# A four-layer graph network on one core: layer 3 in one-pass matmuls behind a run-time check of the adjacency

## The chip, the cores and the metric

The kernel runs on one core of one Trainium2 chip. The metric is device microseconds for one execution. The profile is one further execution, recorded by the hardware profiler; its span is the time between its first and last instruction. Engines are named as in the profile: PE (matrix multiply), PEld (its weight loads), DVE (vector), ACT (scalar, with function tables), POOL (GpSimd) and SP (a queue that issues transfers).

## The reference

A feature matrix x (2708 nodes, 128 features) goes through four graph layers, each on the layer-normed, clipped features and added back to x. The adjacency `adj` is 2708 by 2708 in fp32; it is drawn at random and holds only 0 and 1. Layer 0 is a masked attention, layer 1 a normalised sum over neighbours, layer 2 a mean over neighbours with a batch norm. Layer 3 is the one that the change is about:

```
XW = h @ W ;  s_col = XW @ a[:f] ;  s_row = XW @ a[f:]
den = exp(leaky_relu(s_row[:, None] + s_col[None, :], 0.01))
num = A @ den
att = where(num != 0, den / num, 0)
out = x + A @ (att @ XW)
```

So layer 3 has a product of the adjacency with a 2708 by 2708 matrix, a logarithm and an exponential over all of it, a product with XW, and a last product with the adjacency. The kernel is handed the adjacency as it is (`adj`) and transposed (`adj_t`).

## The kernel before

**Tiles.** Nodes lie in T = 22 tiles of 128 (the last has 20). A row tile of the adjacency is 128 x 2708 fp32, 1354 KB. Columns are worked on in six blocks `E0`: five of 512 and one of 148, each in its own PSUM bank. `product` (layers 1, 2 and the end of 3) walks over the 22 row tiles: for each one, `aggregate` (L209) multiplies the tile by a 128 x 128 stationary matrix into the six banks. The last four tiles (`NLAST`) are walked block by block, so that the `finish` function of a block can begin while the next block is multiplied. Row tiles are fetched by SP into a ring of buffers, so SP waits only for a free buffer.

**Layer 3, tables (L445 to L941).** The kernel does not form the product A @ den row by row. It sorts the nodes by s_row into chunks and the columns by s_col, because inside a chunk the leaky ReLU has one slope. From comparisons, ranks and one-hot matrices (DVE, some PE) it makes index tables: `row_i` (which rows of `adj_t` a step needs), `pre_i` (which pre-summed rows), `xw_i` (which rows of XW). `sums` (L640) streams all 22 tiles of `adj_t` and forms running sums of whole chunks, which are written to DRAM as `pre_d`. `densities` (L910 to L925) fills `dmat`, which holds 44 matrices of 128 x 128.

**Layer 3, the loop (L943 to L990).** It has NE = 22 steps. A step s has two halves. For each half, `fetch` lets POOL gather 126 rows of `adj_t` into partitions 0 to 125 (L457, index `row_i`) and 2 rows of `pre_d` into partitions 126 and 127. The buffers `rows` come from the pool `steps`, which has four. For each of the six blocks, PE multiplies `dmat` of both halves by the two row buffers into a bank (L980), and there are two such banks in turn. ACT takes Ln of the bank (L984), DVE subtracts that from `e` in three pieces (L986), and ACT then takes Exp of all of `e` (L988). `e` itself was begun by DVE at L975, in a buffer that is free once `spread_values` of two steps earlier has read it. `spread_values(s - 1)` (L962) multiplies the `e` of the step before by its gathered XW rows into six accumulators. The order on PE is held by hand: L980 of step s, then L962 of step s - 1.

**Layer 3, the end (L993 to L1030).** The accumulators are turned by PE and scaled into `hn` (L1002); then `product` runs once more over the 22 tiles of `adj_t` with `hn` as the stationary side, and `finish3` adds to x and stores the result.

All matmuls on fp32 data are plain fp32 ones. Each appears in the profile as two records.

Of the kernel before, what the change touches and what calls it, by code (L numbers as in the profile page):

```python
# [10 lines left out]
I32 = mybir.dt.int32  # L11
AF = mybir.ActivationFunctionType
# [5 lines left out]
def kernel(  # L18
# [187 lines left out]
    def aggregate(stationary, moving, accs, start, stop, blocks=range(NB)):  # L206
        for b in blocks:
            lo, hi = E0[b]
            nc.tensor.matmul(accs[b][:, : hi - lo], stationary, moving[:, lo:hi], start=start, stop=stop)  # L209
# [13 lines left out]
    with ExitStack() as stack:  # L223
# [168 lines left out]

        def load_with_turn(t):
            a = kept[t] if t in kept else load_rows(adj, t)
            if t not in kept and turns:
                b = turns.pop(0)
                p = bank()
                turned(p, h2, TILES[b])
                nc.vector.tensor_copy(hT[:, spans(b)], p[:, : len(TILES[b]) * P])
            return a  # L400
# [11 lines left out]
        product(order2, lambda t: h2[:, t, :], load_with_turn, range(NB), finish2)  # L412
        nc.vector.bn_aggr(tot[:, 0:2], st2)
# [15 lines left out]
    CH = P - 2  # L429
# [6 lines left out]
    pre_d = dram.tile([2 * NC, N], F32, name="pre_d")  # L436
# [14 lines left out]
    pre_i = keepers.tile([P, NS], I32, name="pre_i")  # L451
    c_rel = keepers.tile([P, NE], F32, name="c_rel")
    c_exp = keepers.tile([P, NE], F32, name="c_exp")
    r_exp = keepers.tile([P, T], F32, name="r_exp")

    def gather(out, src, idx):
        return nc.gpsimd.indirect_dma_start(  # L457
            out=out,
            out_offset=None,
            in_=src,  # L460
            in_offset=bass.IndirectOffsetOnAxis(ap=idx, axis=0),
        )

# [3 lines left out]
    with tc.tile_pool(name="tab", bufs=1) as tab, tc.tile_pool(name="tabs", bufs=2) as tabs:  # L467
# [27 lines left out]
        nc.vector.memset(first[0:1, :], 1.0)  # L495
        slope_hi = const.tile([P, 1], F32, name="slope_hi")
        nc.vector.tensor_scalar(slope_hi, part, float(CH), -0.99, ALU.is_equal, ALU.mult)
        nc.vector.tensor_scalar_add(slope_hi, slope_hi, 1.0)
        slope_lo = const.tile([P, 1], F32, name="slope_lo")
        nc.vector.tensor_scalar(slope_lo, part, float(CH + 1), 0.99, ALU.is_equal, ALU.mult)  # L500
        nc.vector.tensor_scalar_add(slope_lo, slope_lo, 0.01)
# [371 lines left out]
        nc.vector.tensor_copy(row_i, pick("row_f", ktab[:, NC:]).rearrange("p e h -> p (e h)"))  # L873
        chunk = pick("chunk", lane[:, :NC])
# [19 lines left out]
        first_rows = (hT, row_b)  # L894
        for h in range(2):
            gather(first_rows[h][:CH, :N], adj_t[:, :], row_i[:CH, h : h + 1])

# [29 lines left out]
        for s0 in range(0, FIRST, 4):  # L927
            densities(s0)
        for t in range(NEARLY, T):
            sums(t)  # L930
        for s0 in range(FIRST, NS, 4):
            densities(s0)
        pre_sb = hn.rearrange("p t d -> p (t d)")[:, : 3 * BW].rearrange("p (b i) -> p b i", i=BW)
        with tc.high_priority():
            for b in range(3):
                w = BLK[b][1] - BLK[b][0]
                nc.scalar.copy(pre_sb[: 2 * NC, b, :w], accs[b][: 2 * NC, :w])
                nc.vector.tensor_copy(pre_sb[64 : 64 + 2 * NC, b, :w], accs[b][64 : 64 + 2 * NC, :w])
            flat = hn.rearrange("p t d -> p (t d)")
            for h, queue in enumerate((nc.sync, nc.scalar)):  # L940
                queue.dma_start(pre_d[:, h * HALF : (h + 1) * HALF], flat[64 * h : 64 * h + 2 * NC, :HALF])  # L941

    with tc.tile_pool(name="att", bufs=2) as attp:  # L943

        accs = [acc_bank(b) for b in range(NB)]
        done = {}

        def fetch(s):
            if s < 2:
                a = first_rows[s][:, :N]  # L950
            else:
                a = steps.tile([P, N], F32, tag="rows", name="rows")
                one = gather(a[:CH, :], adj_t[:, :], row_i[:CH, s : s + 1])
                if s < 6:
                    tc.keep_in_program_order(one)
            gather(a[CH:, :], pre_d[:, :], pre_i[0:2, s : s + 1])
            return a
# [7 lines left out]
        for s in range(NE):  # L965
            a2 = [fetch(2 * s + h) for h in range(2)]
            if s >= 3:
                fetch_xw(s)
            xw = xw_s[s % 4]
            m = nc.vector.tensor_scalar_mul(xw, xw, c_exp[:, s : s + 1])  # L970
            if s < 4:
                tc.keep_in_program_order(m)
            e = attp.tile([P, N], F32, tag="e", name="e")
            ln = attp.tile([P, N], F32, tag="ln", name="ln")
            nc.vector.tensor_scalar(e, row_a[:, :N], c_rel[:, s : s + 1], 0.0, ALU.add, ALU.max)  # L975
            beg = 0
            for b, (lo, hi) in enumerate(E0):
                num = bank()
                for h in range(2):
                    m = nc.tensor.matmul(  # L980
                        num[:, : hi - lo], dmat[:, 2 * s + h, :], a2[h][:, lo:hi], start=(h == 0), stop=(h == 1)
                    )
                    tc.keep_in_program_order(m)
                nc.scalar.activation(ln[:, lo:hi], num[:, : hi - lo], AF.Ln, bias=tiny)  # L984
                if b in (2, 4, 5):
                    nc.vector.tensor_sub(e[:, beg:hi], e[:, beg:hi], ln[:, beg:hi])  # L986
                    beg = hi
            nc.scalar.activation(e, e, AF.Exp)  # L988
            done[s] = (xw, e)
            if s:  # L990
                spread_values(s - 1)
        spread_values(NE - 1)


    scale = small.tile([P, T], F32, tag="scale", name="scale")
    nc.vector.scalar_tensor_tensor(scale, deg, 0.0, r_exp, ALU.not_equal, ALU.mult)
    for b in range(NB):
        evacuate(b, yT, accs[b])
        p = bank()
        turned(p, yT, TILES[b], True)  # L1000
        for q, t in enumerate(TILES[b]):
            nc.vector.tensor_scalar_mul(hn[:, t, :], p[:, cols(q)], scale[:, t : t + 1])  # L1002


    late = ctx.enter_context(tc.tile_pool(name="late", bufs=3))
    pools = [steps] * 4 + [late] * 3

    def finish3(b, acc):
        evacuate(b, yT, acc)
        p = bank()  # L1010
        turned(p, yT, TILES[b], True)
        t0 = TILES[b][0]
        f = len([t for t in TILES[b] if t < TF])
        nc.vector.tensor_add(
            xs[:, t0 : t0 + f, :].rearrange("p t d -> p (t d)"),
            xs[:, t0 : t0 + f, :].rearrange("p t d -> p (t d)"),
            p[:, : f * P],
        )
        nc.sync.dma_start(
            out[t0 * P : (t0 + f) * P, :].rearrange("(t p) d -> p t d", p=P), xs[:, t0 : t0 + f, :]  # L1020
        )
        if f < len(TILES[b]):
            nc.vector.tensor_add(xs[:TAIL, TF, :], xs[:TAIL, TF, :], p[:TAIL, cols(f)])
# [37 lines left out]
```

## Time and profile before

| | us |
|---|---|
| median of 3 runs | 1044.93 (1042.61 to 1044.98) |
| the profiled execution | 1046.11 |
| its span | 1044.3 |
| layer 3 loop, first L980 to last L962 | 613.7 to 934.2 |
| end of layer 3, after the loop | 934.2 to 1044.3 |
| mean granted PE clock | 0.972 |

The page gives the busy time of each engine, the same in 40 slices, the transfers, the chain that ended last, and the costliest groups of instructions. A group's row has the line, the engine, the operation, output and inputs by name, shapes and count; then busy microseconds in all, mean nanoseconds of one, and the idle time of that engine just before them with what ended it. A busy PE is not PE at its peak: records overlap, so a mean of one record is longer than the distance between two.

### The profile page before, as it was taken

The page shows a single profiled execution, that of the slowest core. Times are in us where ns is not written, and L with a number is a line of the kernel's source. Part 1 is how long each engine was busy: PE and PEld are TensorE (multiplying, and loading weights), DVE is VectorE, ACT ScalarE, POOL GpSimd, SP SyncE. Part 2 cuts the span into 40 slices and gives each one's busy share as a digit, 9 for nine tenths or more (in the row PEclk, how much of TensorE's full clock was granted, in tenths as well). Part 3 has the DMA queues.
Part 4 walks back from the last instruction along what each step waited for, and adds up shares of the span by engine and source line. Part 5 has one row for each costly group of instructions (what it writes and reads, how often), then busy time and mean ns, then how long its engine had stood idle before and what let it go on. Part 6 is the DMA issues. An engine that isn't in the chain of part 4 may idle for free.

```text
span 1044.3 us, 8022 instructions
## 1 busy us (share of the span) xinstructions
PE 956.5 (92%) x2850; PEld 426.0 (41%) x2850; DVE 461.3 (44%) x869; ACT 440.4 (42%) x579; POOL 165.3 (16%) x156
## 2 busy tenths in 40 slices
PE   4699999999999999966697768999999999999998
PEld 3333333344454544442232123444444444444444
DVE  5799889660004100269787242333333333340002
ACT  4579775230005000168402665665656666640000
POOL 3000001020002000020002041444334443200000
PEclk9899999999999999988899889999999999999999
DMA  8257445258865683074069744655556655569841
GB/s 300 94 213 266 175 165 192 55 225 310 309 229 205 221 302 123 0 320 162 1 257 360 198 163 177 218 192 187 183 200 218 216 181 193 198 249 369 312 170 53
DMA packets 36426, 213.06 MB, mean 204 GB/s; under 512 B 8043, under 2 KB 16923, under 8 KB 17363
## 3 DMA queue, kind: packets, MB, share of 16 engines
q1 hardware_dynamic: 21223, 146.96, 38.0%
q0 software_dynamic: 9152, 62.46, 17.0%
q10 hardware_dynamic: 6011, 3.14, 1.2%
q8 instruction: 22, 0.36, 0.1%
q14 instruction: 18, 0.14, 0.0%
HBM read 209.23 MB, written 3.32 MB: 204 GB/s over the span
## 4 chain that ended last, share of the span: by engine, by line
PE 77%; DVE 9%; ACT 7%; DMA 3%; issue 2%; POOL 1%; ACTq 0%; DVEq 0%; POOLq 0%
PE acc L209 37%; PE bank L980 16%; PE acc L962 10%; PE bank L301 7%; ACT L984 3%; DMA rows<-in_adj_t_dram 2%; PE acc L640 2%; ACT ln L984 1%; POOL rstd L160 1%; DVE bits L577 1%; PE bank L185 1%; DVE st L171 1%; ACT row_a L580 1%; PE bank L917 1%; PE acc L252 1%
## 5 line engine op out<-in xcount | busy, mean ns | idle before, releaser
L980 PE MATMUL bank<-rows,dflat 128*128 128x512 f32 x504 | 201.7, 550 | 10.6 <-ACT ln L984 10.6
L980 PEld LDWEIGHTS bank<-rows,dflat 128*128 128x128 f32 x504 | 90.6, 191 | 119.7 <-issue 91.5
L986 DVE TENSOR_TENSOR e<-e,ln 128x1536 f32<-128x1536 f32 (+2 forms) x66 | 70.5, 1097 | 145.3 <-ACT ln L984 145.3
L984 ACT ACTIVATE ln<-bank,tiny 128x512 f32<-128x512 f32 x132 | 79.4, 634 | 83.4 <-PE bank L980 83.2
L962 PE MATMUL acc<-e,xw 128*128 128x512 f32 (+1 forms) x264 | 103.4, 542 | 0.0
L209 PE MATMUL acc<-rows,hn 128*128 128x512 f32 (+1 forms) x264 | 101.7, 542 | 0.0
L209 PE MATMUL acc<-a,hn 128*128 128x512 f32 (+1 forms) x264 | 100.9, 542 | 0.0
L209 PE MATMUL acc<-a,hs 128*128 128x512 f32 (+1 forms) x228 | 88.1, 542 | 0.0
L286 ACT ACTIVATE tau<-row_a,e_neg,e_lo 128x1536 f32<-128x1536 f32 (+1 forms) x44 | 65.0, 1509 | 37.3 <-PE bank L301 27.4
L204 ACT COPY yT<-acc 128x512 f32<-128x512 f32 x9 | 5.2, 581 | 178.4 <-PE acc L209 174.9
L301 PE MATMUL bank<-tau,pick 128*6 128x512 f32 x180 | 72.6, 542 | 0.0
L962 PEld LDWEIGHTS acc<-e,xw 128*128 128x128 f32 x264 | 48.7, 190 | 52.6 <-issue 47.6
L209 PEld LDWEIGHTS acc<-a,hn 128*128 128x128 f32 x264 | 47.0, 190 | 50.2 <-issue 50.0
L209 PEld LDWEIGHTS acc<-rows,hn 128*128 128x128 f32 x264 | 46.8, 190 | 49.0 <-issue 48.8
L457 POOL DMA_INDIRECT rows<-in_adj_t_dram,row_i x42 | 41.9, 998 | 154.2 <-PE bank L980 147.8
L209 PE MATMUL acc<-yT,hs 128*128 128x512 f32 x132 | 57.6, 574 | 7.8 <-DVE yT L292 7.8
L289 DVE SCALAR_TENSOR_TENSOR tau<-tau,e_hi,a 128x1536 f32<-128x1536 f32 (+1 forms) x38 | 60.5, 1623 | 3.0 <-ACT tau L286 3.0
L975 DVE TENSOR_SCALAR e<-row_a,c_rel 128x2708 f32<-128x2708 f32 x22 | 35.8, 1630 | 57.3 <-PE acc L962 57.2
L209 PEld LDWEIGHTS acc<-a,hs 128*128 128x128 f32 x228 | 41.2, 190 | 45.4 <-issue 45.4
L640 PE MATMUL acc<-rows,wts 128*44 128x452 f32 (+1 forms) x216 | 49.3, 568 | 9.5 <-DMA rows<-in_adj_t_dram 9.4
L457 POOL DMA_INDIRECT xw<-xw_d,xw_i x22 | 41.2, 1873 | 93.7 <-DVE xw_i L841 87.3
L209 PE MATMUL acc<-row_b,hs 128*128 128x512 f32 x132 | 55.5, 553 | 0.0
(343 smaller groups left out, 1048.9 us busy)
## 6 DMA issues: line engine op xcount, KB each, us to landing
a<-in_adj_dram SPq DMA_DIRECT2D x38, 1354.0 KB, 6.5
rows<-in_adj_t_dram SPq DMA_DIRECT2D x38, 1354.0 KB, 7.2
a<-in_adj_t_dram SPq DMA_DIRECT2D x21, 1354.0 KB, 5.8
keep<-in_adj_dram SPq DMA_DIRECT2D x2, 1354.0 KB, 5.8
dflat<-in_adj_t_dram SPq DMA_DIRECT2D x2, 1354.0 KB
xw_d<-hs ACTq DMA_DIRECT2D x1, 1408.0 KB
row_a<-rdeg_d ACTq DMA_DIRECT2D x1, 1354.0 KB
yT<-in_adj_t_dram SPq DMA_DIRECT2D x1, 1354.0 KB, 5.6
```

The costliest lines, as they stand in the source:

```text
L160: nc.gpsimd.tensor_tensor(dst, s[:, :n], neg_half[:, :n], ALU.pow)
L209: nc.tensor.matmul(accs[b][:, : hi - lo], stationary, moving[:, lo:hi], start=start, stop=stop)
L286: nc.scalar.activation(tau[:, :w], row_a[:, h0:h1], AF.Relu, bias=e_neg[:, t : t + 1], scale=e_lo[:, t : t + 1])
L289: nc.vector.scalar_tensor_tensor(tau[:, :w], tau[:, :w], e_hi[:, t : t + 1], a[:, h0:h1], ALU.add, ALU.mult)
L301: nc.tensor.matmul(den[: len(E0), : hi - lo], pick[:, b, :], tau[:, lo - h0 : hi - h0], start=(ndone == 0), stop=(t == T - 1 and b == NB - 1),
L457: return nc.gpsimd.indirect_dma_start(out=out, out_offset=None, in_=src, in_offset=bass.IndirectOffsetOnAxis(ap=idx, axis=0),)
L640: nc.tensor.matmul(accs[b][64 * h : 64 * h + 2 * NC, : hi - lo], wts[:, t, :], a[:, lo:hi], start=(t == 0), stop=(t == T - 1),)
L962: m = nc.tensor.matmul(accs[b][:, : hi - lo], xw, e[:, lo:hi], start=(s == 0), stop=(s == NE - 1))
L975: nc.vector.tensor_scalar(e, row_a[:, :N], c_rel[:, s : s + 1], 0.0, ALU.add, ALU.max)
L980: m = nc.tensor.matmul(num[:, : hi - lo], dmat[:, 2 * s + h, :], a2[h][:, lo:hi], start=(h == 0), stop=(h == 1))
L984: nc.scalar.activation(ln[:, lo:hi], num[:, : hi - lo], AF.Ln, bias=tiny)
L986: nc.vector.tensor_sub(e[:, beg:hi], e[:, beg:hi], ln[:, beg:hi])
```

## The change

1. **A check.** In layer 2's product, each tile of `adj` is also put through `low_bits`: DVE masks the low 12 bits of every word, and ACT sums them into a column of `low`. `low` is reduced during layer 3's tables to `flag`, 0 if all low bits are zero.
2. **A branch.** `flag` is read into a register by every engine ahead of layer 3's loop. If it is 1, `rest(False, ...)` runs; that is the loop and the end of layer 3 in fp32. Otherwise `rest(True, ...)` runs.
3. **One-pass matmuls with halves.** In `rest(True)`, `dmat` of each half is split by DVE into `d_hi` and `d_lo`, both of type float32r (a 32-bit type that the PE multiplies with fewer mantissa bits); the rows are float32r too, and L980's product becomes two float32r matmuls per half. `hn` is split likewise into `y_hi` and `y_lo` for the last product, and each streamed tile of it is copied by DVE into a float32r buffer (`halved`). L962 stays fp32.
4. **Rows.** A half has 124 rows of `adj_t` and 4 of `pre_d` (the pre-summed rows now come in a high and a low part, `pre_hi` and `pre_lo`, made by DVE). The 124 rows are gathered as 112 and 12, with `row_j` (filled by one small transfer on ACT's queue) as the index of the 12. In `rest(True)`, POOL gathers straight into the float32r buffers; only the first four halves are gathered in fp32 into `hT`, `row_b`, `hs` and `yT` ahead of the branch, and copied by `halved`.
5. **Order in the loop.** Rows for step s + 1 are asked for in step s. After each Exp stands a one-column Ln, `again`, which nothing reads. `ln` has one buffer instead of two.

Compiled, the instructions of both sides of the branch follow each other in each engine's program, the fp32 side first.

```diff
     def aggregate(stationary, moving, accs, start, stop, blocks=range(NB)):
+        parts = stationary if isinstance(stationary, list) else [stationary]
         for b in blocks:
             lo, hi = E0[b]
...
+            for i, w in enumerate(parts):
...
+        def low_bits(t, a):
+            junk = (yT, row_b)[t % 2][:, :N]
+            bits = junk.bitcast(I32)
+            m = nc.vector.tensor_scalar(bits, a.bitcast(I32), 0xFFF, None, ALU.bitwise_and)
+            n = nc.scalar.activation(junk, bits, AF.Identity, accum_out=low[:, t : t + 1])
...
-    CH = P - 2
+    CH = P - 4
...
+    def gather_rows(a, s):
+
+        gather(a[:EVEN, :], adj_t[:, :], row_i[:EVEN, s : s + 1])
+        return gather(a[EVEN:CH, :], adj_t[:, :], row_j[: CH - EVEN, s : s + 1])
...
+                high_bits(pre_hi[:w, lo:hi], flat[:w, lo:hi])
+                nc.vector.tensor_sub(pre_lo[:w, lo:hi], flat[:w, lo:hi], pre_hi[:w, lo:hi])
...
+    ahead = {s: fetch(s) for s in range(4)}
...
+        def halved(a):
+
+            r = steps.tile([P, N], F32R, tag="rows", name="rows")
+            tc.keep_in_program_order(nc.vector.tensor_copy(r, a))
+            return r
...
+                if q in rows_of:
+                    r = halved(rows_of.pop(q))
+                else:
+                    r = fetch(q, steps.tile([P, N], F32R, tag="rows", name="rows"))
+                d_hi = attp.tile([P, P], F32R, tag=f"d_hi{h}", name="d_hi")
+                d_lo = attp.tile([P, P], F32R, tag=f"d_lo{h}", name="d_lo")
+                tc.keep_in_program_order(nc.vector.tensor_copy(d_hi, dmat[:, q, :]))
+                tc.keep_in_program_order(nc.vector.tensor_sub(d_lo, dmat[:, q, :], d_hi))
+                terms.setdefault(s, []).extend([(d_hi, r), (d_lo, r)])
...
+                    for i, (d, a) in enumerate(products):
+                        m = nc.tensor.matmul(
+                            num[:, : hi - lo], d, a[:, lo:hi], start=(i == 0), stop=(i == len(products) - 1)
+                        )
...
+                nc.scalar.activation(e, e, AF.Exp)
+
+                again = attp.tile([P, 1], F32, tag="again", name="again")
+                tc.keep_in_program_order(nc.scalar.activation(again, tiny, AF.Ln))
...
+            def load_halved(t):
+                a = spare[t % 4] if t % 4 < 3 else late.tile([P, N], F32, tag="rows", name="rows")
+                return halved(fill(a, adj_t, t))
...
+    some_low = nc.values_load(flag[0:1, 0:1], min_val=0, max_val=1, skip_runtime_bounds_check_because="0 or 1")
+    with tc.If(some_low > 0) as general:
+        with ExitStack() as s3:
+            rest(False, s3)
+    with general.Else():
+        with ExitStack() as s3:
+            rest(True, s3)
```

## Prediction

> **What bounds the kernel now.** I read the page's costliest groups first, then the chain in order of time, then the timeline of one step. The page gives these for layer 3's loop (line, engine, count, then busy us and mean ns of one, then that engine's idle time ahead of it):
>
> ```profile
> L980 PE MATMUL bank<-rows,dflat 128*128 128x512 f32 x504 | 201.7, 550 | 10.6 <-ACT ln L984 10.6
> ...
> L984 ACT ACTIVATE ln<-bank,tiny 128x512 f32<-128x512 f32 x132 | 79.4, 634 | 83.4 <-PE bank L980 83.2
> ...
> L457 POOL DMA_INDIRECT rows<-in_adj_t_dram,row_i x42 | 41.9, 998 | 154.2 <-PE bank L980 147.8
> ```
>
> PE hardly idles ahead of L980; ACT and POOL idle because of it. The chain repeats this with a period of 14.30 us (start, length, what):
>
> ```profile
> 639.27 4.54 PE acc L962 x12
> 643.81 1.73 PE bank L980 x4
> 645.61 1.28 ACT L984
> 647.64 5.92 PE bank L980 x16
> 653.56 4.54 PE acc L962 x12
> ```
>
> So PE sets the step, with one short stop for an ACT table load. One step in the timeline, PE's weight loads left out, shows what stands behind PE:
>
> ```profile
> 702.79 1.28 ACT L984 ACT_TABLE_LOAD   x1 [2.07 <-PE bank L980]
> ...
> 704.83 5.92 PE L980 MATMUL bank<-rows,dflat 128*128 128x512 f32 x16 [0.40 <-ACT ln L984]
> ...
> 710.28 0.96 ACT L984 ACTIVATE ln<-bank,tiny 128x512 f32<-128x512 f32 x2 [1.03 <-PE bank L980]
> ...
> 710.80 0.96 POOL L457 DMA_INDIRECT rows<-in_adj_t_dram,row_i  x1 [7.30 <-PE bank L980]
> 711.00 1.45 DVE L986 TENSOR_TENSOR e<-e,ln 128x1024 f32<-128x1024 f32 x2 [1.68 <-ACT ln L984]
> ...
> 711.26 1.28 ACT L988 ACT_TABLE_LOAD   x1
> ...
> 712.56 2.46 ACT L988 ACTIVATE e<-e 128x2708 f32<-128x2708 f32 x1
> ...
> 715.33 1.63 DVE L975 TENSOR_SCALAR e<-row_a,c_rel 128x2708 f32<-128x2708 f32 x1 [2.88 <-PE acc L962]
> ...
> 715.73 2.07 POOL L457 DMA_INDIRECT xw<-xw_d,xw_i  x1 [0.30 <-issue]
> ```
>
> The Exp table loads right after the last Ln, beside DVE's subtraction; the Ln table loads only once a bank is ready. The windows view gives the loop and the end (busy us of PE, PEld, DVE, ACT, POOL, then PE clock, DMA share, GB/s):
>
> ```profile
> 613.70:934.20 320.50, 309.88 (x793) 141.97 (x794) 112.03 (x112) 191.21 (x201) 117.75 (x102) 0.99 0.56 203
> 934.20:1044.30 110.10, 106.07 (x310) 51.37 (x307) 11.93 (x33) 2.26 (x4) 2.35 (x1) 1.00 0.62 229
> ```
>
> Both are PE-bound with transfers to spare. The transfer view of 935 to 1030 us, in 40 slices, shows what plain loads can reach before PE holds them back, 380 to 430 GB/s:
>
> ```profile
> DMA  8999999998988978896979687897951100000033
> GB/s 255 428 424 433 422 388 387 356 379 333 319 328 278 365 237 365 274 383 192 406 205 429 219 356 253 347 283 310 356 237 41 50 0 0 0 0 0 0 110 93
> ```
>
> **What the Trainium skill says.** "FP8 and Floating Point Precision", TensorE Precision Notes: true fp32 takes four passes, a reduced form reads 4-byte words and truncates them. The trace agrees for the first: a 512-column fp32 matmul is two records 0.428 us apart, 4 x 512 columns in 0.856 us. It has no float32r matmul; the bf16 ones of L586 run five in 1.08 us, 0.216 each, which is my price of one pass. "SBUF — State Buffer", Who interferes with whom: a DVE instruction in a two-port mode shuts GpSimd out. The trace agrees: the xw gather takes 2.07 us beside L975, and 0.94 to 1.18 in the tables. "DMA: Bandwidth & Descriptors", Why a DMA increments its semaphore by 16: a transfer uses the largest number of engines up to 16 that divides its partitions, so 126 rows get 14, 124 would get 4, 112 and 12 get 16 and 12. I only use that the split leaves the gathers no worse spread. "Runtime: NRT & Kernel Launch", Instruction fetch mechanics: a taken branch to a distant target waits for a fetch. No row here shows that wait.
>
> **The loop, part by part.** *PE.* L980 goes from 9.03 us a step (4 x 2 x 2708 columns at 2.4 per ns) to half: per step 20 matmuls of 512 columns at 0.216 and 4 of 148 at about 0.156 (what the weight loads let the 148-column records take now), 4.94 us. L962 stays 4.54. PE's floor is 9.5 us. *ACT* now forms a ring with PE. Let S be the start of block 2. By the latencies above (bank to Ln 0.31, two Ln end to end 0.96): block 4 is ready at S + 2.59, Ln of 4 and 5 end at 3.86, the Exp table at 5.16, DVE's subtraction at about 5.2, Exp at 7.66, the Ln table at 8.96, `again` about 0.2 (the nearest small ACT row, the accumulator read of L274, takes 0.186), the next Ln of block 0 at 9.8, and block 2 again at 9.95. So `again` takes the table load off PE's path, but ACT's own chain is longer than PE's work. *POOL* issues seven gathers a step for five. Now five take 7.0 us from 710.80; the two added ones, priced like the small gather of `pre_d` (0.88 + 0.30), make 9.4, and DVE's extra two-port copies (`d_hi`, about 0.25 each) up to 9.9. *DMA* moves 2 x 128 rows of 10.8 KB plus XW, 2.84 MB a step: 285 GB/s at 9.95 us, where bursts of gathers reach 320 to 357 now. Landing: the last gather of a step is issued about 7.5 us after the products of step s - 1 free its buffer, and lands 6.5 later (median 7.4 from issue), 14.0; it is wanted two periods less one product stage after, 14.3. All four are within 0.5 us of each other, so I add 0.45 for their collisions: **10.4 us a step**. Loop: first block 2 at 3.2, 21 periods 218.4, last step 12.3, together 233.9 for 320.5: **-86.6**. Bounds: PE floor 9.5 (-106); gathers 2 us slower a step, 12.5 (-42). The float32r gathers convert on the way; no gather of before does, so its rate is the widest unknown, and I take the unconverted one.
>
> **The end.** PE falls from 4.54 to about 2.3 us a tile; the loads become the bound at 1.387 MB / 0.42 = 3.3 us. After the last L962, DVE makes `hn` (22 x 0.28) and the halves (6 x about 1), until 13 us; only then come the copies, 1.6 each (L975's form; up to 3.3). Three tiles are loaded ahead, a fourth when `e` is gone; tile 4 is asked for at 15, then 17.2 tiles at 3.3 land by 73; copy, last four tiles block by block 11, tail 4.8: 93 for 110.1, **-17** (-28 if the loads overlap better, -8 if the copies run at half speed).
>
> **Ahead of the loop.** After the last L640: DVE's masks and subtractions +3.2; twice the bytes of `pre_d` +0.5; the branch, during which the gather of `pre_d` runs anyway, and two `halved` copies with four small operations ahead of the first product +4. Transfers bound the tables from 565 to 597 us (share 9 of 10 at some 240 GB/s; PE waits 5.63 us for rows at 586.76), and a third half gathered there adds 1.3 MB, at most 5.4 us; I take 4.5. **+12** (+5 to +20). `row_j` and the flag hide behind the same transfers. The check costs DVE about 1.6 us and ACT 2.64 (L274, the same form) a tile, against 4.54 of PE in layer 2, where DVE is busy 13.6 and ACT 7.1 of 105 us: nothing but a few small operations early on, **+1** (0 to +5, if a `hT` copy queued behind a mask holds a bank).
>
> Sum: -86.6 - 17 + 12 + 1 = -90.6. The profiled execution took 1046.1, so 955.5; it stands 1.2 above the median, so **954 us**.
>
> **Rivals.** (a) *The gathers become the bound.* Seven issues and DVE's port locks, or late landings, make a step 12 to 13.5 us; loop -54 to -22, total about 987 to 1018. For: POOL and landings sit as close as ACT. Against: buffers of two steps, bursts above the rate needed. (b) *Slower: the converting gather.* The other terms sum to -4.6, so the loop breaks even at 325 us, a step of 14.8, which is a gather rate of 192 GB/s. At 170 GB/s a step takes 16.7 us and the whole 1086. For: nothing shows its rate. Against: the gathers now reach 357. (c) *One pass is not one pass.* If a float32r column costs two passes, the step is 9.03 + 4.54, about 13.6 us (-19.5 over the loop), and the end keeps its 100 us of PE behind 13 of DVE (+8): with +13 ahead of it about 1046, no change. (d) *The flag is set* and the fp32 side runs: the step loses its table stop, 13.6, the end stays, and the preamble lacks the copies (+9): about 1035. The data, 0 and 1 with zero low bits, speaks against it.
>
> **How the numbers follow.** Forecast 0.70, (a) 0.18, (b) 0.07, (c) 0.03, (d) 0.02. Forecast, (a) and (d) are faster by over 0.3% (about what a measurement of this kernel can tell from no change), 0.90, less 0.01 for a preamble far above its bound: faster 0.89, within 0.3% (c) 0.03, slower 0.08. Low end: floor of the loop, best end, small preamble: -106 - 28 + 5, 916. High end takes in most of (a): 1010.
>
> **What would show it.** Right: L980 halves to about 100 us; the chain of waits in the loop names ACT (Ln, table, Exp) where it named PE, at 10 to 10.8 us a step; DMA share near 0.8 in the loop; at the end `rows` landings are waited for and loads run near 420 GB/s. Wrong: PE waiting on `rows` from the gathers for microseconds each step; records of L980 0.43 us apart; a gap of over 10 us at the branch; layer 2 longer by more than 5 us.

## The result, and the profile after

The changed kernel takes 1004.92 us (median of 4 runs, 1001.05 to 1006.11); the kernel before took 1044.95 in the same comparison. The ratio is 0.9615, with a 95% interval of 0.9584 to 0.9646: faster by 40 us, where 91 were forecast. Here and below a ratio is of fast runs alone, which leaves out any run more than 1.5% above the fastest of its kernel. The profiled execution took 1006.11 us, its span is 1004.2, and its sections set against the forecast are these:

| section | before | after | change | forecast |
|---|---|---|---|---|
| up to the first product of the loop | 613.7 | 632.4 | +18.7 | +13 |
| loop | 320.5 | 283.3 | -37.2 | -86.6 |
| end | 110.1 | 88.5 | -21.6 | -17 |

So the loop gave less than half of what was expected. The windows view of loop and end shows where to look (busy us of PE, PEld, DVE, ACT, POOL, then PE clock, DMA share, GB/s):

```profile
632.40:915.70 283.30, 236.12 (x795) 142.97 (x795) 135.35 (x203) 199.50 (x224) 157.31 (x142) 0.93 1.04 220
915.70:1004.20 88.50, 68.19 (x308) 53.65 (x306) 51.12 (x67) 2.08 (x4) 2.36 (x1) 0.91 0.76 301
```

The DMA share of the loop went from 0.56 to 1.04 (packet times are summed, so packets in flight together count twice), while the rate rose only from 203 to 220 GB/s. The costliest groups (busy us, mean ns, then the idle time ahead and what ended it):

```profile
L1075 PE MATMUL bank<-rows,d_hi 128*128 128x512 f32 (+1 forms) x264 | 112.7, 431 | 60.9 <-DMA rows<-pre_d,pre_i 33.6
L1079 ACT ACTIVATE ln<-bank,tiny 128x512 f32<-128x512 f32 x132 | 81.8, 638 | 77.4 <-PE bank L1075 75.0
...
L1075 PE MATMUL bank<-rows,d_lo 128*128 128x512 f32 (+1 forms) x264 | 103.1, 401 | 0.0
...
L490 POOL DMA_INDIRECT rows<-pre_d,pre_i x40 | 56.5, 1412 | 14.1 <-issue 11.5
```

PE now stops for 60.9 us ahead of its products. The landing of a gather ends 33.6 us of that, in 18 waits; most of the rest is the wait ahead of the first product (13.7 us) and one in the loop's head (10.8 us). The sum of the two busy figures, 216 us, looks like no saving, but records overlap: in the timeline the 512-column records start 0.23 us apart (792.52, 792.75, 792.98), and a whole product takes 5.14 us. The chain of one step (start, length, what) has no ACT in it:

```profile
780.56 11.41 DMA rows<-pre_d,pre_i
791.97 0.24 issue
792.21 5.14 PE bank L1075 x22
797.35 0.04 issue
797.39 0.84 POOL rows L490
798.24 0.39 issue
798.62 1.05 POOL rows L490
799.67 0.31 issue
799.98 0.90 POOL rows L490
800.87 0.30 issue
801.18 14.20 DMA rows<-in_adj_t_dram,row_i
```

A product frees a buffer, POOL issues the next gathers, and the rows take 11 to 14 us to land. The steps between 700 and 900 us are 12.3 us on average. The transfer view of the same stretch, 40 slices of 5 us, has only its last slice below nine tenths, and no slice above 257 GB/s:

```profile
DMA  9999999999999999999999999999999999999998
GB/s 217 225 221 242 243 221 225 229 225 257 227 217 220 228 244 234 230 231 228 239 248 232 230 231 221 233 225 220 211 228 235 221 234 226 221 251 232 232 230 198
...
q0 software_dynamic: 6751, 45.71, 109.9%
```

From the last line (packets, MB, share of 16 engines) comes the figure that the experiments compare. I call it the **rate of a busy engine**: MB divided by (share x 16 x the stretch). Here it is 45.71 MB / (1.099 x 16 x 200 us) = 13.0 GB/s. For the kernel before, the same view reads

```profile
DMA  9349169178088185194393492590680881852943
GB/s 340 133 154 340 74 212 303 53 241 326 2 294 274 31 338 203 37 366 165 95 337 140 143 344 81 201 340 27 247 319 2 274 289 34 334 208 41 364 163 85
...
q0 software_dynamic: 5818, 39.68, 55.9%
```

which is 39.68 / (0.559 x 16 x 200) = 22.2 GB/s. Packets of the same kind (6.8 KB on average in both) hold an engine 1.7 times as long. The gathers became the bound, as in rival (a), but nothing above says why. Two things in them are new: they convert to float32r, and a half's rows come in three pieces, 112 + 12 + 4, instead of two, 126 + 2.

At the loop's head, not in its steady part, stand a further 9 us: the Exp of the second and of the third step comes 18.9 and 14.8 us after the one before it, where two steady steps take 24.6.

### The profile page after: what moved, and what is told of

Read it like the earlier page. It is cut to its first block, busy times and chain, and to the rows that moved or that the text cites. A ratio compares the mean times of both kernels' runs of the same rounds, so it can differ in the third digit from the quotient of the medians.

```text
span 1004.2 us, 8397 instructions
## 1 busy us (share of the span) xinstructions
PE 849.6 (85%) x2852; PEld 429.9 (43%) x2852; DVE 562.6 (56%) x1030; ACT 503.1 (50%) x646; POOL 209.8 (21%) x201
## 4 chain that ended last, share of the span: by engine, by line
PE 50%; DMA 29%; DVE 11%; POOL 3%; issue 3%; ACT 3%; DVEq 0%; POOLq 0%; ACTq 0%
PE acc L212 29%; DMA rows<-pre_d,pre_i 8%; DMA rows<-in_adj_t_dram,row_i 8%; PE bank L310 7%; DMA rows<-in_adj_t_dram 7%; PE bank L1075 4%; PE acc L689 3%; POOL rows L490 2%; DMA yT<-in_adj_t_dram,row_j 2%; DVE rows L1032 1%; POOL rstd L161 1%; DMA hT<-in_adj_t_dram 1%; DMA rows<-in_adj_t_dram,row_j 1%; ACT row_a L629 1%; DVE bits L626 1%
## 5 line engine op out<-in xcount | busy, mean ns | idle before, releaser
L1075 PE MATMUL bank<-rows,d_hi 128*128 128x512 f32 (+1 forms) x264 | 112.7, 431 | 60.9 <-DMA rows<-pre_d,pre_i 33.6
L1079 ACT ACTIVATE ln<-bank,tiny 128x512 f32<-128x512 f32 x132 | 81.8, 638 | 77.4 <-PE bank L1075 75.0
L1075 PE MATMUL bank<-rows,d_lo 128*128 128x512 f32 (+1 forms) x264 | 103.1, 401 | 0.0
L1075 PEld LDWEIGHTS bank<-rows,d_hi 128*128 128x128 f32 x264 | 54.3, 206 | 96.0 <-issue 58.9
L295 ACT ACTIVATE tau<-row_a,e_neg,e_lo 128x1536 f32<-128x1536 f32 (+1 forms) x44 | 65.1, 1511 | 37.2 <-PE bank L310 27.0
L689 PE MATMUL acc<-rows,wts 128*44 128x452 f32 (+1 forms) x216 | 54.4, 617 | 16.2 <-DMA rows<-in_adj_t_dram 16.2
L212 PE MATMUL acc<-rows,y_hi 128*128 128x512 f32 x132 | 51.5, 394 | 11.5 <-DVE rows L1032 11.5
L490 POOL DMA_INDIRECT rows<-pre_d,pre_i x40 | 56.5, 1412 | 14.1 <-issue 11.5
L1075 PEld LDWEIGHTS bank<-rows,d_lo 128*128 128x128 f32 x264 | 54.5, 207 | 6.9
L1084 ACT ACTIVATE e<-e 128x2708 f32<-128x2708 f32 x22 | 54.2, 2462 | 0.2
```

Of the source, the lines that this page charges most:

```text
L212: nc.tensor.matmul(accs[b][:, : hi - lo], w, moving[:, lo:hi], start=start and i == 0, stop=stop and i == len(parts) - 1,)
L295: nc.scalar.activation(tau[:, :w], row_a[:, h0:h1], AF.Relu, bias=e_neg[:, t : t + 1], scale=e_lo[:, t : t + 1])
L490: return nc.gpsimd.indirect_dma_start(out=out, out_offset=None, in_=src, in_offset=bass.IndirectOffsetOnAxis(ap=idx, axis=0),)
L689: nc.tensor.matmul(accs[b][64 * h : 64 * h + 2 * NC, : hi - lo], wts[:, t, :], a[:, lo:hi], start=(t == 0), stop=(t == T - 1),)
L1075: m = nc.tensor.matmul(num[:, : hi - lo], d, a[:, lo:hi], start=(i == 0), stop=(i == len(products) - 1))
```

## Experiments

**Theory C, conversion:** a gather that converts holds the engines longer. **Theory K, the cut:** 112 and 12 rows are served worse than 126. The first four runs set them against each other, two on the old kernel, two on the new one.

**1. Conversion alone, in the old kernel.**

```
-                a = steps.tile([P, N], F32, tag="rows", name="rows")
+                a = steps.tile([P, N], F32R, tag="rows", name="rows")
...
-            return a
+            return a if s < 2 else a.bitcast(F32)
```

> The kernel before, with one edit: from the third half on the 126 + 2 rows are gathered into float32r buffers (a converting gather) and read by the same fp32 matmuls; the pre-summed rows lose low bits by that. Theory 1 (conversion): the DMA busy share of the loop, 52% before, rises to about 80%, each busy engine moving about 13 GB/s instead of 22; the total stays within 1.5% of 1045 us, since 2.74 MB a step at some 210 to 230 GB/s takes 12 to 13 us and the PE step is 14.6 us. Theory 2 (cut into 112 and 12): share stays near 52%, total within 0.3%.

Ratio 1.0001 (0.9987 to 1.0014). From 700 to 900 us the line reads

```profile
q0 software_dynamic: 5825, 39.76, 59.9%
```

So a busy engine moves 20.7 GB/s, 7% less than before, and not the 13 of theory C, which fails here.

**2. The cut alone, in the old kernel.** The 126 rows come as 112 and 14, with their own index for the 14.

```
-                one = gather(a[:CH, :], adj_t[:, :], row_i[:CH, s : s + 1])
+                gather(a[:112, :], adj_t[:, :], row_i[:112, s : s + 1])
+                one = gather(a[112:CH, :], adj_t[:, :], row_j[: CH - 112, s : s + 1])
```

> The kernel before, with one edit: from the third half on the 126 rows are gathered as 112 and 14, in fp32 without conversion. Theory 1 (conversion): the DMA busy share of the loop stays near 52% and the total near 1045 us (within 0.5%). Theory 2 (the cut): the share rises to about 80% at 13 GB/s for each busy engine; the total stays within 1.5%.

Ratio 1.0039 (1.0021 to 1.0057). Its transfer view of 700 to 900 us:

```profile
DMA  7958939939939949659679599399599499498596
GB/s 204 241 127 256 254 74 271 247 67 280 251 86 253 235 136 254 184 162 256 150 212 238 120 253 251 72 266 238 89 267 240 93 252 242 126 241 210 162 236 169
...
q0 software_dynamic: 5824, 39.75, 79.6%
```

The same bytes now take 79.6% of the engines, 15.6 GB/s for a busy one, and the best slice falls from 366 GB/s (before) to 280. The old kernel hides it, because PE's step of 14.3 us leaves time; most of the 4 us that it loses lies ahead of the loop's first Exp. Theory K holds, on the first test.

**3. The new kernel with 124 rows in one gather.**

```
-        gather(a[:EVEN, :], adj_t[:, :], row_i[:EVEN, s : s + 1])
-        return gather(a[EVEN:CH, :], adj_t[:, :], row_j[: CH - EVEN, s : s + 1])
+        return gather(a[:CH, :], adj_t[:, :], row_i[:CH, s : s + 1])
```

> The 124 rows of a half come as one converting gather instead of 112 and 12. Theory 1 (the conversion makes the DMA engines slow per byte, the cut into 112 and 12 is harmless): engine time per byte stays where it is after (about 13 GB/s for each busy engine in 700 to 900 us), and the loop does not get shorter than 283 us; it gets longer if 124 rows are spread over fewer than 16 engines. Theory 2 (the small gather of 12 rows and its many pieces make the engines slow): with the cut gone each busy engine moves about 22 GB/s again as before the change, the step falls from 12.3 to about 10.4 us, the loop to about 240 us and the total to about 962 us.

1176.15 us, ratio 1.125 (1.115 to 1.1355). The engines are busy 57.8% of the time and yet the loop takes 458 us, some 20 us a step. The prediction's rule gives 124 rows 4 engines, and the slow loop goes with that. But no view shows which engines a gather used, and 57.8% of 16 engines is nine packets in flight on average, so the reason stays open. The run decides nothing between C and K; it shows that the count of rows matters, and that one gather of 124 rows is no way out.

**4. The new kernel without conversion.** All gathers land in fp32 in `hT`, `row_b`, `hs` and `yT` in turn, DVE copies each half, and with that the end's first three tile loads move behind the loop.

```
-                if q in rows_of:
-                    r = halved(rows_of.pop(q))
-                else:
-                    r = fetch(q, steps.tile([P, N], F32R, tag="rows", name="rows"))
+                r = halved(rows_of.pop(q))
+                if q + 4 < NS:
+                    rows_of[q + 4] = fetch(q + 4)
```

> The changed kernel, with all gathers in fp32 into the four buffers hT, row_b, hs and yT in turn, four halves ahead, and every half copied by DVE into a float32r buffer (the same values reach the PE; two more copies of 1.58 us a step on DVE). The end's first three tile loads also move behind the loop with it, since those buffers stay in use. Theory 1 (conversion): the step falls from 12.3 us to 10 to 11 us, now set by PE or by DVE, whose work is about 9.5 us a step; DMA share in the loop falls from over 90% to 60 to 75%; the loop takes about 230 to 245 us, the total 955 to 972 us. Theory 2 (the cut or the many small gathers): DMA stays at over 90% and the step at about 12.3 us; only the loop's head gains, total 990 to 1005 us. Theory 3 (POOL is held by the DVE copies, or DVE is full): step 12 to 14 us with DMA share under 75%, total 990 to 1030 us.

1030.69 us, ratio 0.9851 (0.9813 to 0.9888), which is 26 us slower than the changed kernel and the upper end of theory 3. POOL's groups of 640 to 900 us point to the reason:

```profile
L490 POOL DMA_INDIRECT yT<-in_adj_t_dram,row_i x10 | 19.3, 1935 | 3.0 <-DVE d_hi L1052 1.8 <-issue 1.2
...
L490 POOL DMA_INDIRECT row_b<-in_adj_t_dram,row_j x10 | 15.1, 1509 | 3.0 <-issue 3.0
```

A large gather that takes POOL 0.93 us in the changed kernel takes 1.5 to 1.9 here, a small one 1.4 to 1.5 for 1.00. The two more copies of 1.56 us a step stand beside them, as L975 stood beside the xw gather in the prediction: one gather issued at 722.15 us ends at 725.07, just after a copy that ends at 724.98. The loss is not even. In the steady part three steps in a row take 10.1 to 11.4 us, and then one takes 22 to 24, in which DVE waits for the XW rows, whose gather comes last in a long row on POOL. The rate of a busy engine was 15.8 GB/s without conversion, at a share of 84%, against 13.0 with it at 110%. How much of that is conversion and how much the fuller engines is not separated: with 126 + 2 converting rows the figure is 20.7 at 59.9% (experiment 1) and 19.0 at 87.8% (experiment 5).

**5. The new kernel without the cut.** With 126 + 2 rows, as before the change; the two rows with the low part of the pre-summed values are left out.

```
-    CH = P - 4
+    CH = P - 2
...
-        gather(a[:EVEN, :], adj_t[:, :], row_i[:EVEN, s : s + 1])
-        return gather(a[EVEN:CH, :], adj_t[:, :], row_j[: CH - EVEN, s : s + 1])
+        return gather(a[:CH, :], adj_t[:, :], row_i[:CH, s : s + 1])
```

> The changed kernel with a half of 126 + 2 rows, as before the change, in converting gathers: one of 126 rows and one of 2. The two rows with the low part of the pre-summed values are left out of the computation (the high part stays). Theory cut (the 112 + 12 + 4 pieces make the transfers slow): each busy DMA engine gets back to about 21 GB/s, DMA share in 700 to 900 us falls from 110% to about 80% or less, no waits of POOL on landings, and the step is what PE and ACT set: 10.0 to 10.8 us; the loop 230 to 245 us, the total 955 to 972 us. Theory conversion (float32r landing is slow when the engines are full, though it hid before): the step stays over 11.8 us and the total over 990 us. Rival (POOL or the ring of ACT): DMA share under 90%, step 11 to 12 us, total 970 to 990 us.

972.01 us, ratio 0.9309 (0.928 to 0.9338). These gathers convert, and 128 rows a half arrive as in the changed kernel, in two pieces instead of three. The chain of one step:

```profile
719.99 1.28 ACT L1083
...
721.29 2.46 ACT e L1083
...
723.75 1.19 ACT L1086
...
725.05 0.20 ACT again L1086
725.25 0.59 ACT ln L1078
...
725.88 3.18 PE bank L1074 x12
...
729.08 0.96 ACT ln L1078 x2
```

The next Exp table loads at 730.06: the period is 10.07 us, and the chain is the ring of the prediction (Exp table, Exp, Ln table, `again`, a Ln, PE from the third block on, two Ln) with no transfer in it. From 700 to 860 us the line reads

```profile
q0 software_dynamic: 6302, 42.68, 87.8%
```

which is 19.0 GB/s for a busy engine. This settles the main question: **the cut**, not the conversion, kept the step at 12.3 us. With the cut POOL also issues two gathers a step more, but from 700 to 900 us of the changed kernel POOL was busy for only 122 of 200 us, at a DMA share of 110%. The loop takes 255.9 us, more than the 230 to 245 expected: its head and some late steps still wait for rows.

**6. Is it the ring?** The last kernel without `again`.

> The run with 126 + 2 rows (972 us; the low part of the pre-summed rows left out) without the one-column Ln behind each Exp. By the ring of ACT the Ln table (1.28 us) then loads only when a bank is ready, on the way from PE to ACT: the step grows from 10.07 to between 10.9 and 11.3 us and the total by 14 to 22 us, to about 990 us. If the ring is not what sets the step, no change: 970 to 974 us.

981.99 us. The step is 11.22 us, within the expected 10.9 to 11.3, and ACT's timeline shows the table on PE's path again:

```profile
771.28 1.28 ACT L1078 ACT_TABLE_LOAD   x1 [1.23 <-PE bank L1074]
772.57 1.27 ACT L1078 ACTIVATE ln<-bank,tiny 128x512 f32<-128x512 f32 x2
```

The total rose by 10 us, not by 14 to 22: with `again` late rows stretch some steps beyond 10.07 (from 792 to 858 us five of six take 10.7 to 11.7), and at 11.22 the rows keep up.

**7. and 8. Why are small pieces slow?** The old kernel with one more gather of 14 rows a half, into a scratch buffer: partitions 112 to 125, or every ninth.

```
                 one = gather(a[:CH, :], adj_t[:, :], row_i[:CH, s : s + 1])
+                gather((hT, row_b, yT)[s % 3][112:126, :N], adj_t[:, :], row_j[: CH - 112, s : s + 1])
```

(in the second, `[0:126:9, :N]`)

> The kernel before (126 + 2 rows as it was), and beside each half's gathers one more fp32 gather of 14 rows, in neighbouring partitions 112 to 125 of a scratch buffer that nothing reads. It adds 11% of bytes. Theory place (the small gather is slow because its rows all land in neighbouring partitions and queue for few ports of SBUF): DMA share in 700 to 900 us rises from 56% to over 75%. Theory size (a gather of 14 rows is slow by itself, wherever it lands): also over 75%. If a small gather costs only its bytes: 62%. Time within 1% of 1045 us.

> As the run before, but the extra 14 rows land in every ninth partition (0, 9, ... 117). Theory place: share about 62 to 66%, as its bytes alone. Theory size: over 75%, as with neighbouring partitions. Time within 1% of 1045 us.

Each ran once. In 700 to 900 us the share is 78.3% for 43.61 MB in neighbouring partitions (17.4 GB/s for a busy engine) and 67.2% for 43.68 MB when spread (20.3). Bytes alone give 61.4% (55.9% x 43.61 / 39.68). So of 17 points above the bytes, 11 go with the place. The times, 1059.55 and 1056.29, missed the expected 1%; the steady steps stay at 14.30 us in both, and the loss lies at the loop's head, where the first Exp comes 4 to 7 us later and the second 20 us after the first instead of 14.

**9. and 10. Other cuts.** 117 + 7 and 120 + 4, one number changed (`EVEN`).

> The changed kernel with the 124 rows cut as 117 and 7 instead of 112 and 12; nothing else. If it is the number of rows in the small pieces that all land in neighbouring partitions (7 + 4 a half instead of 12 + 4), the step falls from 12.3 to about 11 us, DMA share in 700 to 860 us from 110% to about 95%, total 970 to 985 us. If the mere presence of a third gather a half costs (its fixed work), the step stays at 12 us or more and the total at 998 to 1008 us.

> As the run before, but cut as 120 and 4: still fewer rows in the small pieces (4 + 4). If their number alone counts, it is faster than 117 and 7: step 10.2 to 10.8 us, total 960 to 975 us. If the large piece matters too[...], it is slower than 117 and 7: share over 100%, step over 11.5 us, total over 988 us.

117 + 7 has a median of 1041.82 us (1020.38 to 1051.48) and a ratio of 0.9838 (0.9758 to 0.9919), 120 + 4 has 1031.4 us (1025.02 to 1040.38) and 0.9878 (0.9824 to 0.9933). The two can't be told apart, and both are slower than 112 + 12 with 0.9615. Fewer rows in the small pieces did not help: 120 + 4, with the fewest, behaved as the second case of its expectation (share 108%, 12.5 GB/s for a busy engine). 117 + 7 was expected to gain and did not; its engines are busy 92% at 14.3 GB/s and PE still waits 40.6 us for rows. Of 117 + 7 I have no explanation.

**11. and 12. The large piece by itself.** In the old kernel, only the large gather, of 112 or 120 rows; the other 14 or 6 rows of a half are left out of the computation. The buffers change as well.

```
-                a = steps.tile([P, N], F32, tag="rows", name="rows")
-                one = gather(a[:CH, :], adj_t[:, :], row_i[:CH, s : s + 1])
+                a = (hT[:, :N], row_b[:, :N], hs.rearrange("p t w -> p (t w)")[:, :N], yT[:, :N])[s % 4]
+                if s in (2, 3):
+                    nc.vector.memset(a[96:, :], 0.0)
+                one = gather(a[:112, :], adj_t[:, :], row_i[:112, s : s + 1])
```

> The kernel before with 112 rows instead of 126 in the gather of every half from the third on, in fp32, into the buffers hT, row_b, hs and yT in turn; 14 rows of a half are left out of the computation (their partitions keep zeros or old rows). Bytes fall by 11%. DMA share over bytes, as before the change: 55.9% of 200 us for 39.68 MB, 1.41 points a MB. If the large piece of 112 rows is itself slow[...]: over 1.8 points a MB in 700 to 900 us. If only the small piece beside it is slow: 1.35 to 1.5. Time near 1045 us, since PE sets the step.

> As the run before with 120 rows[...]; 6 rows of a half are left out. If starts that meet on ports make a large piece slow, this is the worst: over 2.0 points of DMA share a MB. If only small pieces are slow: 1.35 to 1.5. Time near 1045 us.

| large gather beside 2 rows | share, MB in 700 to 900 us | points a MB | GB/s of a busy engine | best slice |
|---|---|---|---|---|
| 126 (before) | 55.9%, 39.68 | 1.41 | 22.2 | 366 |
| 112 | 65.5%, 35.50 | 1.85 | 16.9 | 305 |
| 120 | 87.6%, 37.93 | 2.31 | 13.5 | 237 |

```profile
DMA  9969979979879789799799699699698797896997
GB/s 225 207 142 217 210 149 221 205 151 215 186 179 218 153 197 206 150 220 205 143 232 203 137 230 211 142 227 199 144 223 186 167 222 160 201 208 136 223 212 144
...
q0 software_dynamic: 5376, 37.93, 87.6%
```

That view is of 120 rows: no slice above 237 GB/s. Both figures came where expected, so the large piece is slow even without a small one, in one run of each. No run gathers 126 rows into these buffers; that the buffers matter is unlikely, as 112 + 12 + 4 unconverted rows in them moved 15.8 GB/s for a busy engine (experiment 4) and 112 + 14 + 2 in `rows` 15.6 (experiment 2). (The times, 1062.89 and 1061.4, were to be near 1045; the 16 us lie ahead of the loop's steady steps, which are 14.30 us again.)

**What fits all of this but 117 + 7** is a conflict over the ports of SBUF. The Trainium skill, "SBUF — State Buffer", Door 1: The DMA port swizzle, has 16 ports, each with two groups of four partitions 32 apart. "DMA: Bandwidth & Descriptors", Back-pressure in remote DMA, says of transfers between cores that a saturated port of the destination clogs the path back to the engines that write to it; that it holds for these gathers no run shows. By the first page partitions 112 to 123 lie on three ports, and 14 partitions nine apart on 14 different ones. Suppose that 126, 112 and 120 rows run on 14, 16 and 15 engines, as the prediction's rule gives, and that each engine takes consecutive rows. Then 14 engines that start 9 apart start on 14 different ports, 16 that start 7 apart on 14, and 15 that start 8 apart on 8, and 22.2, 16.9 and 13.5 GB/s have this order. By the same count 117 rows, on 13 engines that start 9 apart, would start on 13 ports and do well, which they didn't. No record here says which engine wrote which row, so this is argued, not shown; shown is that the rate depends on the row count and on the place.

**13. All rows, and no cut.** A gather of 126 rows, the last two placeholders, and then the 4 pre-summed rows over partitions 124 to 127.

```
-                    r = fetch(q, steps.tile([P, N], F32R, tag="rows", name="rows"))
+                    r = steps.tile([P, N], F32R, tag="rows", name="rows")
+                    tc.keep_in_program_order(gather_rows(r, q))
+                    late_pre.append((r, q))
+                if h == 1:
+                    if s >= 3:
+                        fetch_xw(s)
+                    for a, q1 in late_pre:
+                        tc.keep_in_program_order(
+                            gather(a[CH:, :], pre_d[:, :], pre_i[: P - CH, q1 : q1 + 1])
+                        )
...
```

> The changed kernel with the full computation, without the cut: each half gathers 126 rows in one converting gather (the last two are placeholders), and the 4 rows of pre-summed values are gathered over partitions 124 to 127 later, for both halves of a step after both large gathers. The four halves ahead of the branch likewise; the third is gathered after the first two halves' pre-summed rows instead of during the tables. Theory cut: step 10.2 to 11.2 us (POOL waits for a landing ahead of each small gather, which hides in the step), loop 235 to 255 us, tables' end earlier by 3 to 6 us, total 955 to 980 us. Theory conversion: step over 11.8 us, total over 985 us. Rival (the small gathers come too late, PE waits for them): step 11.5 to 13 us with DMA share under 80%, total 980 to 1010 us.

1065.04 us, ratio 1.0172 (1.01 to 1.0244), slower than before the change. The engines work freely (64.3%), but POOL does not. Its timeline (idle ahead and its releaser in brackets):

```profile
771.47 0.96 POOL L490 DMA_INDIRECT xw<-xw_d,xw_i  x1 [0.30 <-issue]
778.38 0.88 POOL L490 DMA_INDIRECT rows<-pre_d,pre_i  x1 [5.95 <-DMA rows<-in_adj_t_dram,row_i]
783.13 1.89 POOL L490 DMA_INDIRECT rows<-pre_d,pre_i  x1 [3.87 <-DMA rows<-in_adj_t_dram,row_i]
785.33 0.97 POOL L490 DMA_INDIRECT rows<-in_adj_t_dram,row_i  x1 [0.30 <-issue]
```

Each small gather overwrites two partitions of a large one, so POOL waits 6 and 4 us for the landings, and the next large gathers are queued behind that: from 768.89 (an earlier large gather) to 785.33 it is 16.4 us, and most steps take about that. I had taken this wait for hidden; it is the rival of the expectation, and beyond it.

**14. and 15. The loop's head.** The end's first three tiles are loaded into `hT`, `row_b` and `hs`; SP issues them as soon as `halved` has copied these, at the loop's start. In these two kernels POOL issues them behind its last gather. The first has 126 + 2 rows, the second is the changed kernel with its cut and its full computation.

```
-                return halved(fill(a, adj_t, t))
+                if t < 3:
+                    tc.keep_in_program_order(nc.gpsimd.dma_start(a, adj_t[t * P : (t + 1) * P, :]))
+                else:
+                    fill(a, adj_t, t)
+                return halved(a)
```

> The run with 126 + 2 rows (972 us; the low part of the pre-summed rows left out), and the end's first three tile loads (4.2 MB) issued by POOL behind its last gather instead of by SP at the loop's head. Theory collision (those loads delay the first gathers: the second step came 23.6 us after the first where 10.1 is the period): the second step comes after 13 to 16 us, loop 10 to 14 us shorter, total 958 to 964 us. Rival (the head waits for the gathers of the third and fourth half, issued late, anyway): second step still 20 us or more, total 968 to 976 us. A part may come back at the end if the three tiles arrive later than they are wanted: 0 to 4 us.

> The changed kernel with its full computation and its cut of 112 and 12, and one edit: the end's first three tile loads (4.2 MB) are issued by POOL behind its last gather instead of by SP at the loop's head. If they are what makes the second and third Exp come 18.9 and 14.8 us after the one before, where 12.3 is the period: the head gets 8 to 12 us shorter, the total 993 to 998 us. If the head is slow because the gathers of the third and fourth half are cut too and come late: gain under 4 us, 1001 us or more.

With 126 + 2: 964.76 us, ratio 0.9234 (0.9209 to 0.9259), 7 us less than experiment 5; the second Exp comes 10.2 us after the first, the loop goes from 255.9 to 249.2 us, and the end takes 88.5 for 88.2. With the cut: 978.70 us, ratio 0.9348 (0.9329 to 0.9367), 26 us less than the changed kernel, more than expected. Three of its runs took 976 to 979 us and two 990 to 992, and the profile is of one at 990.23, so it shows only 16 of the 26 us: there the loop takes 269.8 us for 283.3, the second and third Exp come after 11.4 and 10.1 us, and from 700 us on the gathers are as slow as ever (13.1 GB/s for a busy engine).

So the best version with the full computation is the last one, and 126 + 2 rows without the low part of the pre-summed values is the fastest of all.

## Why the prediction was right or wrong, by its own steps

- **PE: right.** One pass it is: 5.14 us a product where 4.94 was worked out (0.23 us a record for 0.216, 6% more; the loop's granted clock was 0.93 for 0.99, the same 6%). Rivals (c) and (d) are out.
- **ACT's ring: right, but not what bound.** Its 9.95 us measured 10.07 once the cut was gone (experiment 5), and `again` is worth the 1.15 us between 10.07 and 11.22 (experiment 6).
- **DMA: the step that failed.** The prediction wrote "I only use that the split leaves the gathers no worse spread". It took the bursts of the 126-row gathers, 320 to 357 GB/s, for 112 + 12 + 4. In its place the runs showed that the rate goes with the shape: from 700 to 900 us a busy engine moved 13.0 GB/s instead of 22.2, so rows and XW came at 229 GB/s where a step of 9.95 us needs 285. Without the cut the step fell to 10.07 us (experiment 5). Whether the engines rose from 14 to 16 and 12, as the cited rule gives, no view shows, and why the cut shape is slow stays open. The widest unknown was named, but in the wrong place: the conversion, which alone costs 7%.
- **What the loop's missing 49 us are.** In the profiles the early loads at the head cost some 13.5 us (283.3 to 269.8), and the cut another 20.6 (269.8 to 249.2). The split is less sure than that looks. By the medians of the whole kernel, moving the loads and then leaving out the cut gives 26 and 14 us, and in the other order the cut gives 33 and the loads 7; only the sum, 40 us, doesn't depend on the order, and no profile was taken of a run of experiment 15 at 976 to 979. The rest, about 15, is what is left to 233.9: even 126 + 2 rows come late in some steps (PE waits 15.4 us for them) at a DMA share of 0.85. The prediction did name the three tiles loaded ahead, and took them as a gain for the end; that 4.2 MB would be in the way of the first gathers was not asked.
- **The converting gather as the slower rival (b): wrong**, as a mechanism. Rival (a)'s range, 987 to 1018, held the time, with a step of 12.3 us inside its 12 to 13.5, and its reason "late landings" is what the chain shows; POOL's issues were not the bound (122 of 200 us busy). That the total fell into its range is in part luck, as the loss in the head was in no term. In (b), the other terms sum to -4.0 and not to -4.6, which changes nothing that rests on it.
- **Ahead of the loop: +18.7 for +13.** The stop for tiles in the tables' stage, where before it was 22.25 us, is in the changed kernel

```profile
575.19 31.08 DMA rows<-in_adj_t_dram
```

and 21.12 us in the kernel with 126 + 2 rows. It begins where it did before (575.37), so the check in layer 2 shows no cost there. The stop ends 8.7 us later than before, forecast 4.5 and 1; in the profiles of the other kernels with cut gathers of 124 rows (experiments 4, 9, 10 and 15) it ends 2.8 to 9.9 us later, so part of this is spread between executions. The third half's gather and the cut of all three are in it, and since the kernel with 126 + 2 rows also issued its third gather later, the two aren't separated. From there to the first product it is 26.1 us for 16.1, +10 where +7.7 was worked out; the masks cost what was said, `pre_d`'s transfer 5.64 us for 3.28. The branch shows nowhere as a wait of its own.
- **The end: -21.6 for -17, right in kind.** Its transfer view (40 slices of 2.2 us from the loop's end):

```profile
DMA  7900007999999999999999999999999940000993
GB/s 207 404 20 0 0 0 192 433 401 399 433 428 423 428 423 419 428 414 428 419 423 433 404 421 433 409 428 417 409 433 419 419 103 10 0 0 0 247 286 97
```

Loads stop until 13 us, then run at 400 to 433 GB/s, and are done at 71; the prediction had 13, 420 and 73. The last stretch took 17 us for 20.

## What to carry to other kernels

A gather's rate goes with its shape: price a new row count or a new place from a run of that shape, not from the bursts of the old one, and look at the rate of a busy engine where the old bound hides it. When the bound moves from PE to transfers, everything that also uses them has to be placed again; here three loads put at the loop's head for the sake of the end cost 26 us with the cut in place and 7 without it, by the medians. And a wait put on the queue that issues the next transfers, as in experiment 13, cost more than the slow transfers it replaced: 1065.04 us for 1004.92.

## What the runs showed of the hardware that I had not expected

- With the same bytes in a half, unconverted gathers of 126 + 2 rows run at 22.2 GB/s for a busy engine and 112 + 14 + 2 at 15.6; alone beside 2 rows, 112 rows run at 16.9 and 120 at 13.5.
- Fourteen more rows cost 17 points of DMA share above their bytes in neighbouring partitions and 6 when spread over every ninth.
- A gather that converts fp32 to float32r costs 7% of engine time in the 126 + 2 shape; in the cut shape 13.0 GB/s stood against 15.8 without conversion, at shares of 110% and 84%, so that this isn't the conversion's cost alone.
